# A graph network of four layers on one core: 0/1 matrices kept for a second pass, a bias added by TensorE, and 56 scatters moved from the setup into layer 0

## The chip, the cores and the metric

The kernel runs on one core of a Trainium2 chip. The core has TensorE (PE; PEld is its weight load), VectorE (DVE), ScalarE (ACT), GpSimd (POOL) and SyncE (SP). Each engine runs its own queue of instructions in order, and semaphores join the queues. SP, ACT and POOL also issue DMAs. The metric is the device time in microseconds; three runs of the kernel before took 3559.20, 3574.22 and 3567.95 us, with a median of 3567.95 us. In what follows, a time such as "at 655.5" is counted from the start of the one profiled execution.

## What is computed

A network of four graph layers works on 50000 nodes with 64 features and 25000 edges that are sorted by target. Each layer normalises x, applies a ReLU and adds its result to x:

```python
edge_index = jnp.stack([src, dst])
h = jnp.maximum(_layernorm(x, axis=-1), 0.0)
x = x + _L0_gnn_ref(h, edge_index, ...)      # relu(cat(h[src], h[dst]) @ W_msg + b_msg), mean by target, update
h = jnp.maximum(_layernorm(x, axis=-1), 0.0)
x = x + _L1_gnn_ref(h, edge_index, ...)      # normalised sum by target, then a linear layer
h = jnp.maximum(_layernorm(x, axis=-1), 0.0)
x = x + _L2_gnn_ref(h, edge_index, edge_type_8, ...)   # attention by target, then a hidden layer
h = jnp.maximum(_layernorm(x, axis=-1), 0.0)
x = x + _L3_gnn_ref(h, src, dst, edge_weight, ...)     # exp(-t L) h, a Taylor series of sparse products by source
```

Layers 0, 1 and 2 sum over the edges of a target. Layer 3 sums over the edges of a source, so the kernel also needs the edges ordered by source.

## The kernel before

All work is in `fast` (L974). Nodes are handled in NQ = 49 blocks of 1024 (8 columns of 128 nodes). Edges are held 128 to a tile, in NT = 196 tiles. The kernel is written in a tile framework: tiles come from pools, and the framework puts the instructions of every engine into an order of its own. It takes what it expects to be ready first and, of several, what stands first in the program; it also adds the semaphores. So work that stands late in the program can run early: layer 0's first normalisations run at 4 us, ahead of the setup that stands before them. A pool that is opened after another was closed gets its memory, and its tiles wait until that memory is free.

The setup goes through these stages.

- **Pass 1** (L1285 to L1294), once per edge tile: `block_hot` (L1272) compares the tile's source blocks `sblk` with a row of numbers and gives a 0/1 matrix `bh` of 128 x 392 in fp16; two smaller 0/1 matrices follow. Three matmuls add them up to counts per node and per block. `otab` then says which nodes have outgoing edges.
- **Gathers** (L1323): for each of the 196 tiles GpSimd fetches, with one indirect DMA, a flag from `otab` into column 3 of `raw`.
- **Pass 2** (L1374 to L1383): `block_hot` makes the same 0/1 matrix again, two matmuls (L1378, L1380) put the rank of every edge among those of its block into PSUM (`pz`, three buffers), and one DVE operation (L1382) picks the edge's own value into `slot`. From that comes `pf`, the place of every edge in the table `stab`, which is ordered by source.
- **Scatters** (L1402, by the helper at L1018): for each of the 196 tiles GpSimd writes 128 rows of 64 bytes of `raw` to their places `pf` in `stab`, with one indirect DMA.
- **Layer 0's tables** (`layer0_tables`, L1162), a pipeline of three stages over the 49 blocks: `norm` loads and normalises x (L1146 to L1152; ScalarE squares at L1151 and takes roots at L1139), `turn` transposes h on TensorE (L1181), copies it out of PSUM (L1183) and stores it as `h0t`; `product` multiplies by both halves of W_msg into PSUM (`pab`, four buffers, L1196). ScalarE copies one half of the result to `at` (L1197). DVE adds the message bias to the other half (L1198), and `pack` splits it into three bf16 parts (L1099 to L1102). The results go to `atab` (from SP, L1201) and `btab` (from ACT, L1202).
- **The degree work** (L1426 to L1496), mostly on DVE: edge positions `nrs`, keys, degrees of targets, checks.

Then the pools of the setup are closed. `weights` (L2035) loads and prepares the weights of the later layers, and **layer 0** (L2161 to L2229) runs as a pipeline of six stages over the 49 blocks: `fetch` gathers five tiles of `ga` from `atab` on GpSimd (four buffers) and loads `bt`, `cat`, `xt` and `keys` on SP; `hots` builds 0/1 matrices on DVE; `message`, `sums`, `update` and `project` follow. The bias of the update enters by a matmul with three rows of ones (L2005, `bias_in`).

Beside layer 0 runs a generator, `itertools.chain(weights(), load_slots())`. `Pace` (L121) takes 0.1 of a step from it after each stage of each block. `load_slots` (L1906) reads `stab` back in five loads and copies four columns; from these the later lists for layer 3 are built (`lists_pace`, from L1748 on). These lists begin at the end of layer 0. After layer 0 come layers 1, 2 and 3, and at the end GpSimd adds the last terms into `out` (L2720).

Of the kernel before, what the change touches and what calls it, by code (L numbers as in the profile page):

```python
# [23 lines left out]
F16 = mybir.dt.float16  # L24
BF16 = mybir.dt.bfloat16
I32 = mybir.dt.int32
# [43 lines left out]
W3 = ((0, 0), (0, 1), (0, 1), (0, 2), (0, 2), (1, 2), (1, 3), (1, 3), (2, 4), (2, 4), (2, 5), (3, 5), (3, 5), (3, 5))  # L70
SECOND = 3
NKEPT = 14
LEV = 1 << 16
FAR = 1 << 20
NORM = 1.0
# [898 lines left out]
def fast(ctx: ExitStack, tc: tile.TileContext, a: dict, out: bass.AP, flag: bass.AP):  # L974
# [42 lines left out]
    def scatter(tab, src, idx, last):  # L1017
        return nc.gpsimd.indirect_dma_start(  # L1018
            out=tab[:, :], out_offset=IndirectOffsetOnAxis(ap=idx, axis=0),
            in_=src, in_offset=None, bounds_check=last, oob_is_err=False)  # L1020
# [27 lines left out]
    def row_bcast(name, n=D, pool=const):  # L1048
        t = pool.tile([P, n], F32, name="b_" + name)
        src = a[name]  # L1050
        nc.scalar.dma_start(t, bass.AP(tensor=src.tensor, offset=src.offset, ap=[[0, P], [1, n]]))
        return t
# [25 lines left out]
    def along(row, n):  # L1078

        return row[:, None, :].to_broadcast([P, n, row.shape[1]])  # L1080
# [23 lines left out]
    def stacked(pool, src, n, w, name):  # L1104

        x3 = pool.tile([3 * n, 1, 3, w], F32, name=name + "_x")
        nc.vector.tensor_copy(x3[:, 0, 0, :], src)
        h = split(x3)
        which = pool.tile([3 * n, 3], F32, name=name + "_w")
        o = pool.tile([3 * n, w], F32, name=name + "_o")  # L1110
        nc.vector.memset(o, 0.0)
        for k in range(3):

            nc.vector.tensor_scalar(which[:, k:k + 1], pidx[:3 * n], float(k * n), None, op0=OP.is_ge)
            if k < 2:
                nc.vector.tensor_scalar(o[:, 0:1], pidx[:3 * n], float(k * n + n), None, op0=OP.is_lt)
                nc.vector.tensor_mul(which[:, k:k + 1], which[:, k:k + 1], o[:, 0:1])
        nc.vector.tensor_scalar(o, h[:, 0, 0, :], which[:, 0:1], None, op0=OP.mult)
        for k in (1, 2):
            nc.vector.scalar_tensor_tensor(o, h[:, 0, k, :], which[:, k:k + 1], o, op0=OP.mult, op1=OP.add)  # L1120
        b = pool.tile([3 * n, w], BF16, name=name)
        nc.vector.tensor_copy(b, o)
        return b
# [38 lines left out]
    def layer0_tables(hook):  # L1162
        with tc.tile_pool(name="pac", bufs=1) as cp, tc.tile_pool(name="pa", bufs=3) as pool, \
                tc.tile_pool(name="ppa", bufs=1, space=PSUM) as ps:
            wab = cp.tile([P, 2 * D], F32, name="wab")
            for h in range(2):
                for i in range(2):
                    nc.scalar.dma_start(wab[h * D:(h + 1) * D, i * D:(i + 1) * D],
                                        a["L0_gnn_W_msg"][i * D:(i + 1) * D, :])
            bmsg = row_bcast("L0_gnn_b_msg", pool=cp)  # L1170

            def norm(q, s):
                xt = pool.tile([P, 8, D], F32, name="xt")
                load_x(xt, q)
                s.h = pool.tile([P, 8, D], F32, name="h")
                norm_relu(pool, s.h, xt)

            def turn(q, s):
                pt = ps.tile([P, 4, P], F32, name="pt", bufs=2)
                for i in range(4):  # L1180
                    nc.tensor.transpose(pt[:, i, :], s.h[:, 2 * i:2 * i + 2, :].rearrange("p a d -> p (a d)"), ident)  # L1181
                s.tr = pool.tile([P, 4, P], F32, name="tr")
                nc.scalar.activation(s.tr, pt, AF.Copy)  # L1183
                for h in range(2):
                    nc.scalar.dma_start(
                        h0t[:, 1024 * q:1024 * q + 1024].rearrange("f (i h n) -> f h i n", i=4, h=2)[:, h],
                        s.tr[h * D:(h + 1) * D])

            def product(q, s):
                at = pool.tile([P, 8, D], F32, name="at")  # L1190
                b3 = pool.tile([P, 8, 3, D], F32, name="b3")
                for h in range(2):
                    pab = ps.tile([P, 4, 2 * D], F32, name="pab", bufs=4)
                    for i in range(4):
                        r = slice(h * D, h * D + D)
                        nc.tensor.matmul(pab[:, i, :], s.tr[r, i, :], wab[r, :], start=True, stop=True)  # L1196
                    nc.scalar.activation(at[:, h::2, :], pab[:, :, :D], AF.Copy)  # L1197
                    nc.vector.tensor_add(b3[:, h::2, 0, :], pab[:, :, D:], along(bmsg, 4))  # L1198
                bt = pool.tile([P, 8, BW], BF16, name="bt")
                pack(b3, bt.rearrange("p b (k d) -> p b k d", k=3))  # L1200
                nc.sync.dma_start(nodes(atab, q), at)  # L1201
                nc.scalar.dma_start(nodes(btab, q), bt)  # L1202

            pipeline(range(NQ), (norm, turn, product), hook)


# [9 lines left out]
    with tc.tile_pool(name="emp", bufs=1) as pool:  # L1216
        none = pool.tile([P, NQ, PW], I32, name="none")
        nc.vector.memset(none, 0)
        nc.vector.memset(none[:, :, 0:1], -1)
        for tab, n in [(stab, TL)] + [(lrow[k], c) for k, c in CAP.items() if k > 3]:  # L1220
            for t in range(0, n, NQ):
                m = min(NQ, n - t)
                nc.scalar.dma_start(tab.rearrange("(p t) f -> p t f", p=P)[:, t:t + m, :], none[:, :m, :])

    with tc.tile_pool(name="so", bufs=1) as sp, tc.tile_pool(name="sw", bufs=4) as sw:
        def load_e(name, dt, pad):
# [42 lines left out]
        nc.vector.memset(spike, 0.0)  # L1269
        nc.vector.memset(spike[:, HT2 - 1:HT2], 1.0)  # L1270

        def block_hot(t):  # L1272
            b = sw.tile([P, BK], F16, name="bh")
            nc.vector.tensor_scalar(b, it16[:, :BK], sblk[:, t:t + 1], None, op0=OP.is_equal)
            return b

# [89 lines left out]
        with tc.tile_pool(name="ps2", bufs=2, space=PSUM) as ps:  # L1366
            st = block_slots(outd, ps, "s")
            for i in range(2):
                pp = ps.tile([HT2, BK], F32, name="pp")
                if i:  # L1370
                    nc.tensor.matmul(pp, ones[:HT2, :HT2], hist[:, 0, :], start=True, stop=False)
                nc.tensor.matmul(pp, above[:HT2, :HT2], hist[:, i, :], start=(i == 0), stop=True)
                nc.vector.tensor_add(pre16[:, i, :], pp, st[:HT2, :])
            for t in range(NT):  # L1374
                h, u = divmod(t, HT2)
                b = block_hot(t)
                pz = ps.tile([P, BK], F32, name="pz", bufs=3)
                nc.tensor.matmul(pz, ident16[:HT2, u:u + 1].to_broadcast([HT2, P]), pre16[:, h, :],  # L1378
                                 start=True, stop=False)
                nc.tensor.matmul(pz, above16, b, start=False, stop=True)  # L1380
                junk = sw.tile([P, BK], F32, name="junk", bufs=2)
                nc.vector.scalar_tensor_tensor(junk, rowi[:, :BK], sblk[:, t:t + 1], pz, op0=OP.is_equal,  # L1382
                                               op1=OP.mult, accum_out=slot[:, t:t + 1])  # L1383

        nc.vector.tensor_scalar(slot, slot, 0.0, float(FAR), op0=OP.max, op1=OP.min)
        si, s1, s2 = (sp.tile([P, NT], I32, name=f"slot{i}") for i in range(3))
# [12 lines left out]
        nc.vector.scalar_tensor_tensor(s2, srct, float(N), s2, op0=OP.is_ge, op1=OP.max)  # L1399
        pf = sp.tile([P, NT], I32, name="pf")  # L1400
        nc.vector.scalar_tensor_tensor(pf, s2, float(FAR), s1, op0=OP.mult, op1=OP.add)
        for t in range(NT):  # L1402
            put = scatter(stab, raw[:, t, :], pf[:, t:t + 1], P * TL - 1)
            if t:
                tc.declare_no_dep(put.ins, group="slots", reason="rows are distinct")
            tc.add_to_no_dep_group("slots", put.ins)


        rl = sp.tile([NQ, RW, 3], I32, name="rl")
# [493 lines left out]

    cols = [lw.tile([P, BK], I32, name=f"lcol{i}")[:, :TL] for i in range(4)]

    def load_slots():  # L1906

        for t0 in range(0, TL, NQ):
            part = lw.tile([P, NQ, PW], I32, name="lpart")
            nc.sync.dma_start(part, stab.rearrange("(p t) f -> p t f", p=P)[:, t0:t0 + NQ, :])  # L1910
            yield
            for i, c in enumerate(cols):
                nc.vector.tensor_copy(c[:, t0:t0 + NQ], part[:, :, i])
        nc.vector.tensor_scalar(skey.rearrange("p (q i) -> p q i", i=5), rowi[:, :NQ, None].to_broadcast([P, NQ, 5]),
                                -1024.0, None, op0=OP.mult)
        nc.vector.tensor_add(skey, skey, cols[0])
        nc.vector.tensor_copy(swgt.bitcast(I32), cols[2])
        nc.vector.tensor_copy(sptr, cols[1])
        yield
# [241 lines left out]
    with tc.tile_pool(name="l0c", bufs=1) as cp, tc.tile_pool(name="l0", bufs=2) as pool, \  # L2161
# [61 lines left out]
            nc.scalar.dma_start(nodes(x1tab, q), s.x1)  # L2223
            nc.sync.dma_start(nodes(g1tab, q), g)

        work = Pace(itertools.chain(weights(), load_slots()), 0.1)
        next(work.work)
        lists_pace.edge = 5.0
        pipeline(range(NQ), (fetch, hots, message, sums, update, project), work, lists_pace, False)  # L2229
# [557 lines left out]
```

## Time and profile before

| what | value |
|---|---|
| median of three runs | 3567.95 us |
| the profiled execution | 3569.77 us |
| its span, first to last instruction | 3568.0 us |
| mean granted TensorE clock | 0.693 |
| DVE busy | 2620.7 us (73%) |
| PE busy | 2492.4 us (70%) |
| POOL busy | 2070.2 us (58%) |
| ACT busy | 1328.5 us (37%) |
| pass 1 | 22 to 131 us |
| pass 2 | 138 to 314 us |
| layer 0's tables | 314 to 587 us |
| degree work on DVE | 587 to 647.5 us |
| layer 0, first message matmul | 684.7 us |
| first use of the lists' columns | 1094.6 us |

Lines of the profile are read so. A row of the stretches view has the stretch and its length, then for each engine the busy time and, in brackets, the number of instructions; then the granted TensorE clock (1.00 is full), the share of the DMA engines that was busy, and GB/s. A line of the timeline has the start, the duration, the engine, the line of the program, the operation, `out<-in`, the shape and the number of merged instructions; a bracket at its end gives the idle time before it and what ended that. "q" behind an engine (SPq, ACTq) marks the engine's sequencer, which issues DMAs. In the view of a tile the three durations of a group are the least, the median and the greatest, in ns. The busy slices of the page cut the span in 40 equal parts of 89 us; a digit is the busy share in tenths.

### The profile page before, as it was taken

The numbers are of one execution on the slowest core, as the hardware profiler recorded it, in microseconds if no ns is written. First come the engines' busy times: TensorE is split into PE (matmuls) and PEld (weight loads), VectorE is DVE, ScalarE is ACT, GpSimd is POOL, SyncE is SP. The second block draws the span as 40 slices with busy tenths as digits, with TensorE's granted clock in tenths as the row PEclk, the third lists the DMA queues.
The fourth block names the chain that finished last, engine by engine and source line by source line (L and its number), as shares of the span: only waits on it lengthen the run. The fifth ranks groups of instructions, "written<-read, shape, count | busy, mean of one in ns | idle before, by whom it ended". The sixth has DMA issues, their size and how long they took to land. (4 is left out here: it accounts for less than half of the span.)

```text
span 3568.0 us, 62333 instructions
## 1 busy us (share of the span) xinstructions
PE 2492.4 (70%) x21184; PEld 1729.4 (48%) x21184; DVE 2620.7 (73%) x8434; ACT 1328.5 (37%) x2962; POOL 2070.2 (58%) x1955
## 2 busy tenths in 40 slices
PE   7898675399987673477669779889888554356620
PEld 3324565266665452355446445555554443356520
DVE  9999998699998882488677877777878576456410
ACT  0002553144442262377204326646667333333000
POOL 0377777655550477665374127665430787775786
PEclk9755555699996575688657667777779775567555
DMA  1003783487771362478654234343233646377221
GB/s 54 6 4 90 205 234 123 110 224 212 211 200 44 90 197 75 130 234 243 188 145 124 62 90 132 111 122 110 80 94 101 211 139 193 96 216 213 45 26 12
DMA packets 530638, 463.35 MB, mean 130 GB/s; under 512 B 281171, under 2 KB 387954, under 8 KB 530180
## 3 DMA queue, kind: packets, MB, share of 16 engines
q1 hardware_dynamic: 365012, 269.33, 26.5%
q10 hardware_dynamic: 93408, 139.47, 11.3%
q0 software_dynamic: 71888, 50.46, 7.6%
q8 instruction: 169, 2.77, 0.3%
q14 instruction: 161, 1.32, 0.1%
HBM read 226.23 MB, written 233.89 MB: 129 GB/s over the span
## 5 line engine op out<-in xcount | busy, mean ns | idle before, releaser
L1013 POOL DMA_INDIRECT kvg<-kvtab,nrs x245 | 260.6, 1064 | 307.6 <-DVE es L2329 184.0
L1013 POOL DMA_INDIRECT gt<-g1tab,nrs x245 | 243.6, 994 | 238.6 <-DVE lhot L1791 110.6
L1013 POOL DMA_INDIRECT y<-h3tab,sptr x245 | 276.8, 1130 | 138.9 <-issue 68.0
L1013 POOL DMA_INDIRECT ga<-atab,nrs x245 | 250.3, 1022 | 170.4 <-DVE z L2190 60.5
L1991 PEld LDWEIGHTS <-soh 128*128 128x128 bf16 x4410 | 221.7, 117 | 237.0 <-issue 221.8
L1013 POOL DMA_INDIRECT raw<-otab,nrd x196 | 193.4, 987 | 191.9 <-DVE bad L1159 132.5
L1981 PE MATMUL pa<-soh,m 128*64 128x256 bf16 (+3 forms) x1764 | 238.9, 348 | 25.2 <-DVE m L1093 11.6
L1018 POOL DMA_INDIRECT stab<-raw,pf x196 | 207.3, 1058 | 59.8 <-issue 59.8
L1013 POOL DMA_INDIRECT lgot<-nmap,ldst x183 | 190.1, 1039 | 75.3 <-issue 52.8
L1991 PE MATMUL po<-g,soh 128*128 128x64 bf16 x2205 | 123.3, 215 | 145.5 <-DVE g L1093 143.0
L1950 DVE TENSOR_SCALAR soh<-it,key 128x512 bf16<-128x512 f16 (+2 forms) x735 | 210.7, 332 | 1.8 <-PE pa L1981 1.6
L1991 PE MATMUL po<-y,soh 128*128 128x64 bf16 x2205 | 122.3, 228 | 125.9 <-DVE y L1093 65.4
L2272 PE MATMUL pp<-wkv,tr 64*128 64x256 f32 x784 | 151.2, 496 | 52.4 <-ACT tr L2001 52.1
L1013 POOL DMA_INDIRECT y<-ftab,ldst x140 | 138.9, 992 | 75.0 <-issue 45.7
L1093 DVE TENSOR_TENSOR y<-y 128x320 f32<-128x320 f32 (+1 forms) x196 | 75.6, 389 | 140.6 <-ACT y L2617 116.3
L1942 DVE TENSOR_SCALAR noh<-keys,pblk 128x256 bf16<-128x256 f16 (+1 forms) x784 | 176.0, 286 | 2.8 <-DMA keys<-ktab 2.7
L1196 PE MATMUL pab<-wab,tr 64*128 64x128 f32 x784 | 150.3, 437 | 32.5 <-ACT tr L1183 32.5
L1981 PEld LDWEIGHTS <-m 128*64 128x64 bf16 x1764 | 118.0, 119 | 97.9 <-issue 32.5
L1196 PEld LDWEIGHTS pab<-wab,tr 64*128 64x128 f32 x784 | 136.3, 324 | 51.5 <-ACT tr L1183 51.5
L2338 PE MATMUL pe<-qt,noh 128*128 128x64 bf16 x2205 | 157.7, 231 | 0.3 <-DVE noh L1942 0.2
L2720 POOL DMA_INDIRECT out<-y,lnode x85 | 132.4, 1558 | 38.3 <-issue 24.4
L2617 ACT ACTIVATE y<-y,swgt 128x64 f32<-128x64 f32 x245 | 82.2, 345 | 176.6 <-DMA y<-h3tab,sptr 161.1
(607 smaller groups left out, 7496.8 us busy)
## 6 DMA issues: line engine op xcount, KB each, us to landing
kvtab<-kv SPq DMA_DIRECT2D x49, 512.0 KB
ftab<-f ACTq DMA_DIRECT2D x98, 256.0 KB
xt<-in_x SPq DMA_DIRECT2D x96, 256.0 KB
btab<-bt ACTq DMA_DIRECT2D x49, 384.0 KB
bt<-btab SPq DMA_DIRECT2D x49, 384.0 KB
qtab<-qt ACTq DMA_DIRECT2D x49, 384.0 KB
qt<-qtab SPq DMA_DIRECT2D x49, 384.0 KB
xs<-xstab SPq DMA_DIRECT2D x70, 256.0 KB
```

Of the source, the lines that this page charges most:

```text
L1013: return nc.gpsimd.indirect_dma_start(out=dst, out_offset=None, in_=tab[:, :], in_offset=IndirectOffsetOnAxis(ap=idx, axis=0))
L1018: return nc.gpsimd.indirect_dma_start(out=tab[:, :], out_offset=IndirectOffsetOnAxis(ap=idx, axis=0), in_=src, in_offset=None, bounds_chec ...
L1093: nc.vector.tensor_sub(x3[:, :, k, :], x3[:, :, k - 1, :], h[:, :, k - 1, :])
L1196: nc.tensor.matmul(pab[:, i, :], s.tr[r, i, :], wab[r, :], start=True, stop=True)
L1942: nc.vector.tensor_scalar(s.noh[:, j, :n * P], s.keys[:, t0 * P:(t0 + n) * P], pblk[:, j:j + 1], None, op0=OP.is_equal)
L1950: nc.vector.tensor_scalar(oh[:, OHW[i]:OHW[i + 1]], it16[:, b0 * P:(b0 + n) * P], keys[:, q, i:i + 1], None, op0=OP.is_equal)
L1981: nc.tensor.matmul(o, l, r, start=(k == 0), stop=(k == len(t) - 1))
L1991: nc.tensor.matmul(po[:, j, :], oh[:, c:c + P], msg[:, i, k, :], start=(not started and i == t0 and k == 0), stop=(end and (not started or ...
L2272: nc.tensor.matmul(pp[:, i, :], s.tr[r, 2 * k + i, :], wkv[r, :], start=True, stop=True)
L2338: nc.tensor.matmul(pe[:, i, :], s.noh[:, j, c:c + P], s.qt[:, j, k, :], start=False, stop=(j == b0 + nb - 1 and k == 2))
L2617: nc.scalar.activation(y3[:, i, 0, :], s.y[:, i, :], AF.Copy, scale=swgt[:, 5 * q + i:5 * q + i + 1])
L2720: st = nc.gpsimd.indirect_dma_start(out=out[:, :], out_offset=IndirectOffsetOnAxis(ap=s.node[:, t:t + 1], axis=0), in_=sums[k][:, t, :], i ...
```

## The change

Three things are changed.

1. `block_hot` keeps its matrix in pass 1 for the first HELD = 112 tiles, in one tile `held` of 128 x 112 x 392 fp16, and pass 2 takes it from there. The memory is given back after pass 2, before layer 0's tables are opened.
2. In the tables the message bias is put into PSUM by one matmul per half block: three rows of ones times three bf16 rows of the bias, with zeros in the half that gets none. The four products of the half block are added to it, and ScalarE copies the result to `b3` in place of DVE's addition. The bias rows are prepared by `stacked` (L1104), a memset and a copy.
3. Of the 196 scatters into `stab`, the setup issues 140. The rows and places of the last LATER = 56 tiles are stored to DRAM by two DMAs on ACT's queue. `load_slots` loads them again on SP, at the start, into layer 0's memory, issues the 56 scatters one for each step, and only then reads `stab`. The pace goes from 0.1 to 0.34 of a step.

```diff
+HELD = 112
+LATER = 56
...
-            bmsg = row_bcast("L0_gnn_b_msg", pool=cp)
+            b1 = stacked(cp, row_bcast("L0_gnn_b_msg", pool=cp)[:3, :], 1, D, "bmsg")
+            bmsg = cp.tile([3, 4, 2, D], BF16, name="bmsg4")
+            nc.vector.memset(bmsg, 0.0)
+            nc.vector.tensor_copy(bmsg[:, :, 1, :], b1[:, None, :].to_broadcast([3, 4, D]))
+            bmsg = bmsg.rearrange("p b k d -> p (b k d)")
...
                     pab = ps.tile([P, 4, 2 * D], F32, name="pab", bufs=4)
+                    nc.tensor.matmul(pab.rearrange("p b d -> p (b d)"), ones3, bmsg, start=True, stop=False)
                     for i in range(4):
                         r = slice(h * D, h * D + D)
-                        nc.tensor.matmul(pab[:, i, :], s.tr[r, i, :], wab[r, :], start=True, stop=True)
+                        nc.tensor.matmul(pab[:, i, :], s.tr[r, i, :], wab[r, :], start=False, stop=(i == 3))
                     nc.scalar.activation(at[:, h::2, :], pab[:, :, :D], AF.Copy)
-                    nc.vector.tensor_add(b3[:, h::2, 0, :], pab[:, :, D:], along(bmsg, 4))
+                    nc.scalar.activation(b3[:, h::2, 0, :], pab[:, :, D:], AF.Copy)
...
+    def to_slots_by_source(t, rows, places):
+        put = scatter(stab, rows, places, P * TL - 1)
+        if t:
+            tc.declare_no_dep(put.ins, group="slots", reason="rows are distinct")
+        tc.add_to_no_dep_group("slots", put.ins)
+
+    later = [dram.tile([P, LATER * n], I32, name=nm) for nm, n in (("lraw", PW), ("lpf", 1))]
...
-        def block_hot(t):
-            b = sw.tile([P, BK], F16, name="bh")
+        held_pool = ExitStack()
+        held = held_pool.enter_context(tc.tile_pool(name="held", bufs=1)).tile([P, HELD, BK], F16, name="held")
+
+        def block_hot(t, again=False):
+            if t < HELD:
+                b = held[:, t, :]
+                if again:
+                    return b
+            else:
+                b = sw.tile([P, BK], F16, name="bh")
             nc.vector.tensor_scalar(b, it16[:, :BK], sblk[:, t:t + 1], None, op0=OP.is_equal)
             return b
...
-                b = block_hot(t)
+                b = block_hot(t, True)
...
+        held_pool.close()
...
-        for t in range(NT):
-            put = scatter(stab, raw[:, t, :], pf[:, t:t + 1], P * TL - 1)
-            if t:
-                tc.declare_no_dep(put.ins, group="slots", reason="rows are distinct")
-            tc.add_to_no_dep_group("slots", put.ins)
+        for t in range(NT - LATER):
+            to_slots_by_source(t, raw[:, t, :], pf[:, t:t + 1])
+        nc.scalar.dma_start(later[0], raw[:, NT - LATER:, :].rearrange("p t f -> p (t f)"))
+        nc.scalar.dma_start(later[1], pf[:, NT - LATER:])
...
-    def load_slots():
+    def load_slots(pool):
 
+        rows, places = pool.tile([P, LATER, PW], I32, name="rows"), pool.tile([P, LATER], I32, name="places")
+        nc.sync.dma_start(rows.rearrange("p t f -> p (t f)"), later[0])
+        nc.sync.dma_start(places, later[1])
+        yield
+        for t in range(LATER):
+            to_slots_by_source(NT - LATER + t, rows[:, t, :], places[:, t:t + 1])
+            yield
...
-        work = Pace(itertools.chain(weights(), load_slots()), 0.1)
+        work = Pace(itertools.chain(weights(), load_slots(cp)), 0.34)
```

## The prediction, made before the changed kernel was run

> **What bounds the kernel now.** I read the busy slices of the page first, then the busy time of chosen stretches, then the timeline and the list of waits inside those that the change touches. The chain that ended last reaches back only to the additions into `out` (L2720) and the stage before them; the change touches nothing there. What it can move is the start of layer 0, and all later stages hang on that through x.
>
> ```profile
> DVE  9999998699998882488677877777878576456410
> POOL 0377777655550477665374127665430787775786
> PEclk9755555699996575688657667777779775567555
> ```
>
> ```profile
> core 0: us, PE busy (x) PEld busy (x) DVE busy (x) ACT busy (x) POOL busy (x), PEclk, DMA share, GB/s
> 22.00:131.00 109.00, 108.11 (x588) 47.73 (x588) 109.00 (x599) 1.24 (x3) 0.00 (x0) 1.00 0.02 5
> 152.00:314.00 162.00, 149.39 (x367) 45.24 (x365) 154.34 (x557) 1.28 (x1) 122.67 (x130) 0.50 0.03 4
> 340.00:590.00 250.00, 188.01 (x916) 159.20 (x916) 223.76 (x457) 141.48 (x313) 192.67 (x189) 0.50 0.73 215
> 590.00:655.50 65.50, 15.19 (x247) 14.61 (x247) 54.09 (x158) 1.43 (x3) 51.53 (x43) 0.50 0.03 6
> 690.00:1090.00 400.00, 366.69 (x4212) 275.07 (x4210) 381.12 (x1154) 180.87 (x455) 229.41 (x224) 0.97 0.74 208
> ```
>
> The rows are pass 1, pass 2, layer 0's tables, the degree work, layer 0. DVE paces the first two; the tables have no full engine. Layer 0 starts when two chains are done: DVE's (its last setup work at 647.5) and GpSimd's (196 gathers from 134.4 to 387.6, then 196 scatters to 654.3). The later ends the setup's memory, and all queues restart together:
>
> ```profile
> 653.35 0.97 POOL L1018 DMA_INDIRECT stab<-raw,pf  x1 [0.30 <-issue]
> 655.61 0.11 DVE L1111 MEMSET bupd_o<- 3x64 f32 x1 [8.11 <-DMA stab<-raw,pf]
> 655.59 0.57 SPq L2053 DMA_DIRECT2D wkv<-in_L_gnn_Wk  x1
> 677.05 0.36 SPq L2175 DMA_DIRECT2D bt<-btab  x1
> ```
>
> So GpSimd is the bound by only 8 us over DVE. From 655.5 to the first message matmul at 684.7 SP issues the weight loads and then layer 0's first loads; that stretch stays.
>
> **Pass 2 (saves).**
>
> ```profile
> 300.62 0.62 DVE L1382 SCALAR_TENSOR_TENSOR junk<-rowi,f_sblk,pz 128x392 f32<-128x392 f32 x1
> 301.17 0.86 DVE L1274 TENSOR_SCALAR bh<-it,f_sblk 128x392 f16<-128x392 f16 x3
> 302.15 0.62 DVE L1382 SCALAR_TENSOR_TENSOR junk<-rowi,f_sblk,pz 128x392 f32<-128x392 f32 x1
> ```
>
> Durations overlap, so I count from start to start: 0.55 us from one L1382 to the next (300.62 to 301.17), 0.98 for three 0/1 matrices, 0.327 each, 0.873 a tile. For 112 tiles L1274 goes: 112 x 0.327 = **-36.6**. Late next is TensorE, whose matmuls here (L1380) start 0.33 apart at clock 0.50, 0.66 a tile; at that the saving is 112 x (0.873-0.66) = -23.9. In pass 1 a gapless stream got clock 1.00 and 0.17 a matmul, so I take -36.6.
>
> **What the kept matrices push away.** `held` is 112 x 784 B = 88 KB a partition. I expect the table stage's tiles to get that memory only after its last read. Before, DVE did six reductions, six scalings and three subtractions for the first blocks while it waited at the start:
>
> ```profile
> 3.99 0.69 DVE L1146 TENSOR_REDUCE ln_s<-xt 128x8 f32<-128x512 f32 x1 [1.22 <-DMA xt<-in_x]
> ```
>
> At 0.60, 0.10 and 0.60 apart that is **+6** on DVE's path (0 if the memory does not collide). The bias rows need some 18 small DVE operations; like those of `bupd` (0.05 to 0.1 apart) **+2**.
>
> **Tables (unclear sign).** DVE loses 98 additions L1198, 0.375 apart: 37 us. ScalarE gains 98 copies of 0.38: 141 of 250 busy becomes 178, hidden while PSUM copies do not stand ahead of the turn copy L1183; if they do, 0.38 a block, 19 us. TensorE gains 98 matmuls. Its steady rhythm:
>
> ```profile
> 539.93 3.09 PE L1196 MATMUL pab<-wab,tr 64*128 64x128 f32 x16 [0.69 <-ACT tr L1183]
> 542.96 1.11 PE L1181 MATMUL pt<-ident,h 128*128 128x128 f32 x4
> 544.76 3.10 PE L1196 MATMUL pab<-wab,tr 64*128 64x128 f32 x16 [0.69 <-ACT tr L1183]
> ```
>
> 4.82 us a block, 49 x 4.82 = 236 of the stage's 273; in the rest TensorE waited for DVE's h (33 us by the waits). A bias matmul has this shape in layer 0:
>
> ```profile
> L2005 PE MATMUL po<-bupd,ones x49: 371/385/601, 664.2 to 1151.2; 3*128 3x512 bf16 x49
> ```
>
> A block's two cost from 0 (in the 0.69 gap) to 1.20 (the cold maximum). I take 0.385 each, half hidden: 49 x 0.385 = +19. DVE's lost work gives back some of TensorE's 33 us; I take 15, since DVE's long reciprocals and scans still stand in its queue. Net **+4**.
>
> At clock 0.50 these matmuls are dear. The Trainium skill, "TensorE: Matmul & The Clock Gate", Part 1, says the clock rises to full after about 3.4 us of sustained work; our row has 0.50 at 75% busy. With the rule the second rival below would become the forecast, 3508 in place of 3538.
>
> **GpSimd and queues.** Setup keeps 140 scatters at (654.3-387.6)/196 = 1.361: 387.6 + 190.5 = 578, no longer last. DVE's chain ends at 647.5-36.6+6+2+4 = 622.9, so the release moves from 655.5 to 622.9: **-32.6**. ScalarE's queue gets two stores of the last 56 tiles, which wait for the last gather (387.6) and hold the table work behind them; 0 if they are queued about when the gathers end.
>
> **Layer 0.** 56 scatters come into GpSimd's queue among 245 gathers, about two a block after the rows are loaded:
>
> ```profile
> 809.50 0.94 POOL L1013 DMA_INDIRECT ga<-atab,nrs  x1 [0.30 <-issue]
> 812.88 1.42 POOL L1013 DMA_INDIRECT ga<-atab,nrs  x1 [2.44 <-DVE noh L1942]
> ```
>
> It waits 2.0 to 2.4 us a block for a free buffer, 100 us between 700 and 1100, and the scatters need 56 x 1.361 = 76. The gathers are up to four blocks ahead. I take **+3**; if the scatters do not fall into the waits, a block takes 5 x 1.31 + 2.07 x 1.361 = 9.4 instead of 8.6, 27 blocks, +21. DVE, 95% busy there, gets nothing. SP gets two loads; the five loads of the slot table now wait on SP for the last scatter, with layer 0's loads behind them, covered by four buffers. Before they were issued by 962, and the lists begin at 1094.6: room.
>
> Sum: -32.6 + 3 = -29.6. The profiled execution took 3569.8 (span 3568.0 and 1.8 around it): 3540. The median of the runs is 1.8 lower, so **3538**.
>
> **Rivals.**
> - *TensorE becomes the tables' bound at half clock.* For: 188 of 250 busy at 0.50, a rhythm with 0.69 spare. With both matmuls added, 4.82+0.77 = 5.59, x 49 = 274, and 15 us of waits: 289, +16; at 0.60 each, 6.02, 295 and 10: +32. Total 3558 to 3574. Against: DVE's 37 us.
> - *TensorE fills up and gets the full clock.* Pass 1 shows the state, 690 to 1090 too. Then transfers bound the tables: a block moves 1.18 MB (x in, h0t, atab, btab; 256, 256, 256 and 384 KB in the list of DMA issues), at the 245 GB/s seen from 400 to 440 that is 4.8 us, 236 in all, -37 instead of +4: 3497. With three quarters of that I price it at 3508. GpSimd's 578 is the floor, 3495. Against: 0.50 for 250 us on end.
> - *The stores block ScalarE* (slower). Place: its queue, before the tables. If they stand ahead of the first table work, that begins at 390 and not at 285: 390+277+60 = 727, +72 on the release, 3643. It is slower than before once ScalarE idles over 30 us. Against: DVE's free 2.6 us at 631.6 was not filled by the L1111 and L2166 memsets that wait for the scatters, so the planned order does not count on GpSimd much earlier than it is. The Trainium skill, "DMA: Bandwidth & Descriptors", on the anatomy of one DMA, says that a transfer's semaphore wait is held by the issuing sequencer, which speaks for this rival; here ACT's loads L2012 stood until 655.62.
> - *GpSimd bounds layer 0*: 3538+18 = 3556.
>
> **Chances.** Forecast 0.40 (3524 to 3554); full clock 0.24; TensorE bound 0.20; blocked ScalarE 0.07; GpSimd 0.09. The range 3500 to 3582 leaves out the slower cases (0.10) and the fast end of the full clock (some 0.06). Half a per cent, about what a measurement can tell from no change, is 18 us. Faster: 0.37 + 0.24 + 0.02 = 0.63. Slower: 0.06 of the block and 0.04 of a TensorE bound with further stalls = 0.10. Same: 0.27.
>
> **What would show it.** L1382 0.55 apart for 112 tiles and the tables starting near 285; a table rhythm near 5.0 us (over 5.6 or under 4.7 is a rival); the last setup scatter near 578; all queues restarting near 623 on DVE and not on GpSimd; layer 0 at 8.6 us a block. It is wrong if ScalarE stands before 390, or if the lists wait for the slot table.

## The result and the profile after

The changed kernel is **slower**: 3732.9 us (median of 4 runs, 3718.4 to 3733.6) against 3568.7 of the kernel before, ratio 1.045 [1.043, 1.047]. The forecast was 3538, range 3500 to 3582. The profiled execution took 3718.4 us, 148.6 more than that of before; it is the fastest of the four, the others took 3732 to 3734 us. On some chips the kernel before itself took 4680 to 4749 us; every ratio below is with runs of the kernel before on the same chip.

Most of pass 2's gain is there. The busy slices (DVE, POOL, PEclk) and the same stretches as before: pass 1, pass 2, a new one, the tables.

```profile
DVE  9990577776799878248867787787878667556410
POOL 0477770057665146766547313757531378766786
PEclk9955555578899757668855766777778775567555
```

```profile
core 0: us, PE busy (x) PEld busy (x) DVE busy (x) ACT busy (x) POOL busy (x), PEclk, DMA share, GB/s
22.00:131.00 109.00, 106.54 (x580) 46.89 (x579) 109.00 (x601) 1.88 (x4) 1.15 (x1) 1.00 0.01 3
152.00:272.00 120.00, 108.56 (x337) 36.67 (x335) 116.50 (x425) 0.00 (x0) 90.74 (x97) 0.71 0.07 10
279.00:392.00 113.00, 1.86 (x4) 0.41 (x4) 0.69 (x3) 0.00 (x0) 85.40 (x91) 0.50 0.03 6
395.00:690.00 295.00, 252.63 (x1065) 179.39 (x1067) 213.88 (x407) 176.66 (x434) 135.94 (x125) 0.50 0.69 194
```

The fourth slice of DVE is 0: from 279 to 392 us DVE and TensorE work 0.69 and 1.86 us, ScalarE nothing. Only GpSimd goes on, with its gathers and the first scatters. ScalarE's timeline says why ("q" marks its DMA issues):

```profile
197.80 2.50 ACTq L1170 DMA_DIRECT2D wab<-in_L_gnn_W_msg  x4
200.34 0.59 ACTq L1053 DMA_DIRECT2D b_L_gnn_b_msg<-in_L_gnn_b_msg  x1
376.67 0.33 ACTq L1429 DMA_DIRECT2D lraw<-raw  x1
392.13 0.33 ACTq L1430 DMA_DIRECT2D lpf<-pf  x1
392.50 0.63 ACT L1153 ACTIVATE ln_sq<-ln_xc 128x512 f32<-128x512 f32 x1 [264.65 <-DMA rl<-fields]
```

The two stores stand ahead of the tables' first square. The first goes at 376.7, after the last gather (issued at 374.0); the second 15.5 us later, which the profile puts down to SP's `rl` loads. SP's queue was held too: 58 of its 98 `rl` loads were out by 225, then it stood 153.3 us, put down to the first store, and went on at 379.2. Before, these loads ran from 133.6 to 253.7 without such a stop. Why loads on SP wait for that store is not shown. DVE waits behind ScalarE:

```profile
393.16 0.69 DVE L1140 TENSOR_REDUCE ln_v<-ln_sq 128x8 f32<-128x512 f32 x1 [113.47 <-ACT ln_sq L1153]
```

A second hole is in layer 0. SP issues nothing for 64 us, while `keys`, `xt` and `bt` of the next blocks stand behind the first load of the slot table (SP's timeline):

```profile
878.80 0.39 SPq L2206 DMA_DIRECT2D bt<-btab  x1
879.52 1.10 SPq L2060 DMA_DIRECT2D cat<-h0t  x2
944.32 0.33 SPq L1941 DMA_DIRECT2D lpart<-stab  x1
944.74 0.39 SPq L1966 DMA_DIRECT2D keys<-ktab  x1
945.21 0.38 SPq L1070 DMA_DIRECT2D xt<-in_x  x1
```

The last scatter was issued at 942.2. In the order of GpSimd's queue the 56 late scatters do not stand two a block, but 2, 10, 12, 12, 12 and 8 between the gathers of one block and the next, so that the gathers of five blocks lie 18, 23, 22, 22 and 17 us apart.

The ledger, in us of the profiled executions. The restart is the first weight load on SP, the rest is all that comes after layer 0's last message matmul:

| | before | after | difference |
|---|---|---|---|
| pass 2, first to last pick of a slot | 138.1 to 313.3 | 133.3 to 271.5 | 175.2 to 138.2: -37.0 |
| tables, first to last product | 318.6 to 583.9 | 397.6 to 691.4 | 265.3 to 293.8: +28.5 |
| last scatter of the setup | 653.4 | 567.7 | |
| restart | 655.6 | 754.6 | +99.0 |
| first message matmul | 684.7 | 784.9 | **+100.2** |
| layer 0, first to last message matmul | 439.0 | 494.1 | **+55.1** |
| rest of the span | 2444.3 | 2437.6 | -6.7 |

The last row is not read as an effect: in the profiles of the eight kernels that ran on chips of this kind it lies between 2427 and 2455 us.

### The profile page after: what moved, and what is told of

The parts are those of the page before. It is cut to its first block, busy times and chain, and to the rows that moved or that the text cites. A ratio compares the mean times of both kernels' runs of the same rounds, so it can differ in the third digit from the quotient of the medians.

```text
span 3716.6 us, 62517 instructions
## 1 busy us (share of the span) xinstructions
PE 2516.1 (68%) x21282; PEld 1737.3 (47%) x21282; DVE 2561.4 (69%) x8241; ACT 1350.2 (36%) x3060; POOL 2047.0 (55%) x1955
## 5 line engine op out<-in xcount | busy, mean ns | idle before, releaser
L1015 POOL DMA_INDIRECT raw<-otab,nrd x196 | 185.7, 947 | 187.3 <-DVE st_s L1370 127.9
L1140 DVE TENSOR_REDUCE ln_v<-ln_sq 128x8 f32<-128x512 f32 x147 | 99.9, 681 | 201.1 <-ACT ln_sq L1153 200.7
L1153 ACT ACTIVATE ln_sq<-ln_xc 128x512 f32<-128x512 f32 x147 | 92.0, 626 | 341.3 <-DMA rl<-fields 264.7
L1020 POOL DMA_INDIRECT stab<-raw,pf x140 | 151.1, 1079 | 42.6 <-issue 42.6
```

The costliest lines, as they stand in the source:

```text
L1015: return nc.gpsimd.indirect_dma_start(out=dst, out_offset=None, in_=tab[:, :], in_offset=IndirectOffsetOnAxis(ap=idx, axis=0))
L1020: return nc.gpsimd.indirect_dma_start(out=tab[:, :], out_offset=IndirectOffsetOnAxis(ap=idx, axis=0), in_=src, in_offset=None, bounds_chec ...
L1140: nc.vector.tensor_reduce(v, sq, AX.X, OP.add)
L1153: nc.scalar.activation(sq, xc, AF.Square)
```

## The experiments

**Theory.** ScalarE's queue (113 us of idling), SP's wait with GpSimd's bunched scatters (55), and the bias in the tables (22 to 28, put down to TensorE's matmuls) lost far more than pass 2 gained. The rivals are stated with each run.

### Stores off ScalarE's queue

```diff
-        nc.scalar.dma_start(later[0], raw[:, NT - LATER:, :].rearrange("p t f -> p (t f)"))
-        nc.scalar.dma_start(later[1], pf[:, NT - LATER:])
+        nc.gpsimd.dma_start(later[0], raw[:, NT - LATER:, :].rearrange("p t f -> p (t f)"))
+        nc.gpsimd.dma_start(later[1], pf[:, NT - LATER:])
```

> The kernel with the two stores on GpSimd's queue and the late scatters as the changed kernel has them, where the kernel before takes about 3575 us. The tied kernel took 3562. If the bunched scatters and SP's wait behind them make the stall of layer 0, this one has it again: 35 to 45 us more, 3597 to 3607 us. Rival (the stall of the changed kernel came from something that the late tables brought): no stall, within 8 us of 3562.

Measured: 3604.8 us (two runs, 3597.2 and 3612.4), ratio 1.0096 [1.0059, 1.0132] to a kernel before of 3567.2. ScalarE's timeline:

```profile
200.14 0.59 ACTq L1053 DMA_DIRECT2D b_L_gnn_b_msg<-in_L_gnn_b_msg  x1
278.55 0.63 ACT L1153 ACTIVATE ln_sq<-ln_xc 128x512 f32<-128x512 f32 x1 [150.70 <-DVE ln_xc L1151]
```

The first square comes at 278.6 and no longer at 392.5, and waits for DVE, which comes from pass 2. The restart comes at 633.7: the stores' place alone cost 754.6 - 633.7 = **121 us**. Memory did not hold the tables until 392: SP issued the first `xt` loads at 197.6, once the last kept matrix had been read. SP's `rl` loads have no stop here. Layer 0 still takes 492.3 us, so its stall is independent of the late tables.

### Slot-table loads off SP's queue as well

```diff
-            nc.sync.dma_start(part, stab.rearrange("(p t) f -> p t f", p=P)[:, t0:t0 + NQ, :])
+            nc.gpsimd.dma_start(part, stab.rearrange("(p t) f -> p t f", p=P)[:, t0:t0 + NQ, :])
```

> The same with the five loads of the slot table on GpSimd's queue, so that the wait for the last scatter no longer stands on SP ahead of layer 0's loads; the scatters stay bunched. If SP's wait alone makes the stall: near the tied kernel, 3560 to 3567 us. If the bunched scatters starve layer 0 through GpSimd's queue: 25 to 45 us above it, 3587 to 3607 us.

Measured: 3586.2 us, ratio 1.0043 [1.0027, 1.0058], on the chip of the run before. Layer 0 takes 478.0 us: 14 of the 53 are SP's wait, 39 stay. They are four blocks of 13.5, 20.8, 22.5 and 17.1 us by their stores of `g1tab`, against 8.6 otherwise: 73.9 - 34.4 = 39.5. There GpSimd is the bound; its own waits between 740 and 840 are the 0.3 us before each DMA (the three largest groups):

```profile
POOL stab L1020 <- issue: 13.4, 44, 0.3
POOL ga L1015 <- issue: 8.8, 29, 0.3
POOL ga L1015 <- DMA ga<-atab,nrs: 0.6, 2, 0.3
```

SP's wait alone did not make the stall; the bunched scatters are the larger part.

### Scatters tied to the gathers

The stores on GpSimd's queue, the slot-table loads on SP again, and each late scatter placed behind the gathers that precede it in the program:

```diff
+            with tc.issue_after(fetched[-1].ins):
+                to_slots_by_source(NT - LATER + t, rows[:, t, :], places[:, t:t + 1])
...
-                gather(s.ga[:, i, :], atab, nrs[:, q, i:i + 1])
+                fetched.append(gather(s.ga[:, i, :], atab, nrs[:, q, i:i + 1]))
```

> The kernel with the two stores on GpSimd's queue, and the late scatters tied: each may not stand in GpSimd's order ahead of the gathers of layer 0 that precede it in the program, so that two stand between the gathers of two blocks and not ten to twelve. Where the kernel before takes 3568 us: if the bunching starves layer 0, its stall goes from 50 us to under 15 and the time is 3560 to 3565 us, 35 to 40 below the kernel with the bunched scatters; rival (the wait on SP for the last scatter alone): the wait moves to the place of the last scatter and stays, within 10 us of that kernel's 3600. Where the kernel before takes over 4700 us, the same differences against 4745.

Measured: 3562.3 us, ratio 0.9964 [0.9936, 0.9992] to a kernel before of 3577.8. Layer 0 takes 459.8 us. I first took the 21 us over 439 for GpSimd's two scatters a block, since that is the price of the prediction's worse case. SP's timeline shows another place:

```profile
931.93 0.32 SPq L2258 DMA_DIRECT2D g1tab<-g  x1
...
941.09 0.32 SPq L2258 DMA_DIRECT2D g1tab<-g  x1
...
945.68 0.33 SPq L1969 DMA_DIRECT2D keys<-ktab  x1
973.12 0.33 SPq L1944 DMA_DIRECT2D lpart<-stab  x1
973.54 0.38 SPq L2209 DMA_DIRECT2D bt<-btab  x1
974.02 0.82 SPq L2258 DMA_DIRECT2D g1tab<-g  x1
```

Up to 941 the blocks take 9.0 to 9.2 and 8.2 us in turn, 8.65 on average, almost as before (8.6): two scatters a block fit. Then SP stands 27 us before the first load of the slot table. The blocks after it are 32.9, 6.1 and 6.6 us apart, 45.6 for three and not 25.8: +19.8, nearly the whole loss.

### The kept matrices alone

Bias on DVE, all 196 scatters in the setup, the old pace.

```diff
-LATER = 56
+LATER = 0
...
```

> Only the kept matrices, all 196 scatters in the setup, bias on DVE, the old pace; the kernel before at about 3577. If GpSimd's chain of gathers and scatters is the bound, which pass 2 does not shorten: the last scatter near 650, restart 5 to 10 us earlier, 3567 to 3573 us. Rival (the chain moves with pass 2, since the places come 40 us earlier): 3537 us.

Measured: 3563.3 us, ratio 0.9991 [0.9974, 1.0008]. The timeline at the restart:

```profile
650.00 0.97 POOL L1020 DMA_INDIRECT stab<-raw,pf  x1 [0.30 <-issue]
652.23 0.56 SPq L2069 DMA_DIRECT2D wkv<-in_L_gnn_Wk  x1
652.24 0.11 DVE L1113 MEMSET bupd_o<- 3x64 f32 x1 [42.56 <-DMA stab<-raw,pf]
```

DVE has been idle for 42.6 us when GpSimd's last scatter ends, 34.5 more than before the change (8.1): nearly all that pass 2 gains turns into a wait for GpSimd. The scatters must leave the setup for pass 2 to count.

### Kept in SBUF, tied, bias on DVE

The last 24 tiles are gathered into a tile that outlives the setup, so there is neither a store nor a load; the places are copied by one DVE operation.

```diff
+LATER = 24
...
+            gather(raw[:, t, 3:4] if k < 0 else rows[:, k, 3:4], otab, nrd[:, t:t + 1])
...
+        nc.vector.tensor_copy(places, pf[:, NT - LATER:])
...
```

> A kernel made from the findings: matrices kept for 112 tiles, bias on DVE, 24 tiles scattered late from a tile that is kept in SBUF (no stores and no loads), tied to the gathers of layer 0, two a block. If the bias matmuls make the tables 297 us long, they take 276 here, DVE is done near 617 and the last of 172 scatters ends near 624: the restart comes near 625 and the time is 25 to 33 us below the kernel before, 3544 to 3552 where that takes 3577. Rival (the tables are as long without the bias matmuls, since something else bounds them): restart near 638, 3558 to 3566 us.

Measured: 3546.4 us, ratio 0.9932 [0.9905, 0.9959], below the kernel before (3567.2 here). Tables 280.1 to 545.2 = 265.1 us, as long as before the change; restart at 619.4. With the bias on TensorE they took 286.8 (stores on GpSimd's queue). The stretch from 400 to 540 us, first with the bias on TensorE, then without:

```profile
400.00:540.00 140.00, 130.60 (x549) 91.95 (x547) 102.40 (x196) 89.77 (x222) 109.23 (x102) 0.50 0.77 213
```

```profile
400.00:540.00 140.00, 107.59 (x520) 90.78 (x520) 124.31 (x255) 80.71 (x181) 107.71 (x107) 0.50 0.76 217
```

With the bias on TensorE that engine is 93% busy and without it 77%, at a clock of 0.50 in both. It looks like the bound; its timeline with the bias (stores on GpSimd's queue) is close to gapless:

```profile
500.84 3.09 PE L1203 MATMUL pab<-wab,tr 64*128 64x128 f32 x16 [0.15 <-ACT tr L1189]
503.86 0.60 PE L1200 MATMUL pab<-bmsg,ones 3*128 3x512 bf16 x1
504.58 1.12 PE L1187 MATMUL pt<-ident,h 128*128 128x128 f32 x4
505.63 0.60 PE L1200 MATMUL pab<-bmsg,ones 3*128 3x512 bf16 x1
506.38 3.09 PE L1203 MATMUL pab<-wab,tr 64*128 64x128 f32 x16 [0.15 <-ACT tr L1189]
```

506.38 - 500.84 = 5.54 us a block, where it was 4.82: two bias matmuls of 0.60, of which one fits into the gap where TensorE waits for the turn copy (0.69 before, 0.15 left). But ScalarE's queue is as full. Its three stores a block are issued there, and the next root comes only when they are out:

```profile
506.36 0.58 ACTq L1191 DMA_DIRECT2D h0t<-tr  x1
507.12 0.47 ACTq L1209 DMA_DIRECT2D btab<-bt  x1
507.64 0.60 ACTq L1191 DMA_DIRECT2D h0t<-tr  x1
508.29 0.30 ACT L1141 ACTIVATE ln_v<-ln_v,epsc 128x8 f32<-128x8 f32 x1 [1.44 <-issue]
```

Of the 140 us ScalarE is busy for 89.8, stands 31.3 in this way and waits 18 for other engines; with the bias on DVE it waits 57. This run takes the matmuls and the copies away together, so it cannot say which of the two made the tables longer. Copies without matmuls follow further down.

### The wait on SP taken away

The kernel just shown, with the five loads of the slot table six blocks later in SP's order.

```diff
+        for _ in range(12):
+            yield
...
+            with tc.issue_after(loaded[-1].ins):
+                nc.sync.dma_start(part, stab.rearrange("(p t) f -> p t f", p=P)[:, t0:t0 + NQ, :])
...
+            loaded.append(nc.sync.dma_start(s.bt, nodes(btab, q)))
```

> The kernel with 24 late scatters at two a block, and the five loads of the slot table six blocks later in SP's order (tied to a block's own load on SP), so that the last scatter is long done when SP comes to the first of them. Seen so far in that kernel, where the kernel before takes 3567 us: the blocks with two scatters run at 8.6 us as without, and the one loss of layer 0 is 7 to 10 us where SP stands 13 us at the first load. If SP's wait is all that the late scatters cost, layer 0 goes from 449 to 439 to 441 us and the time from 3546 to 3536 to 3539, 28 to 31 below the kernel before. Rival (the scatters themselves cost 0.4 us each, the loss only comes out later): layer 0 stays near 449, 3544 to 3550 us.

Measured: **3536.9 us**, ratio 0.9895 [0.9872, 0.9917] to a kernel before of 3570.4: the best of all. SP's timeline has no hole at the first load, and the blocks around it stay 8.2 and 9.0 apart:

```profile
843.17 0.32 SPq L2254 DMA_DIRECT2D g1tab<-g  x1
845.40 0.54 SPq L1940 DMA_DIRECT2D lpart<-stab  x1
...
851.36 0.32 SPq L2254 DMA_DIRECT2D g1tab<-g  x1
...
860.34 0.32 SPq L2254 DMA_DIRECT2D g1tab<-g  x1
```

Layer 0 takes 444.0 us, against 448.7 with the wait. Of the 8 to 10 expected 5 came back. The time fell within what was expected, but its interval and that of the kernel with the wait overlap a little, so the pair is told apart by the timeline rather than by the times. The two profiled executions even stand the other way round (3534.3 with the wait, 3543.0 without): a restart 3 us later and a rest of the span of 2444.2 against 2434.0 hide the 5.

### Runs on chips with a slower setup

Twelve runs fell on chips where the kernel before takes 4680 to 4749 us. There the setup is another one. DVE's timeline of pass 2 with the stores on GpSimd's queue:

```profile
303.32 0.62 DVE L1406 SCALAR_TENSOR_TENSOR junk<-rowi,f_sblk,pz 128x392 f32<-128x392 f32 x1 [4.96 <-remote]
308.92 0.62 DVE L1406 SCALAR_TENSOR_TENSOR junk<-rowi,f_sblk,pz 128x392 f32<-128x392 f32 x1 [4.97 <-remote]
```

A tile takes 5.6 us while GpSimd gathers (until 378 us), and pass 2 ends at 505; the gathers are then long done, so that a store that waits for them holds nobody. What is tested of the stores and of layer 0 is hidden, and all ratios lie between 0.995 and 1.004. The first four, on one chip:

> The changed kernel with one edit: the two stores of the last 56 tiles are issued from GpSimd's queue, where they stand behind the gathers anyway, and no longer from ScalarE's. Queue theory (ScalarE stood before the tables because the store of raw waits for the last gather): the tables begin near 281 us in place of 395 and, at their 295 us, end near 576; with the 61 us from there to the restart of all queues, that comes near 637; the stall of layer 0 around 880 to 944 stays at about 50 us; 3600 us. Rival (the tables began late because their tiles wait for memory, that of the kept matrices, or for SP's loads): they still begin near 395, 3715 to 3735 us.

> The kernel with the two stores on GpSimd's queue, and the message bias added by DVE again as before the change. Theory (the two bias matmuls of a block make TensorE the bound of the tables at half clock): the tables take 276 us as before and not 295, so 19 us less than the kernel with the stores on GpSimd's queue, near 3581 us. Rival (the longer tables come from elsewhere, DVE's additions cost as much as TensorE's matmuls): within 5 us of that kernel, near 3600.

> The kernel with the two stores on GpSimd's queue, and the five loads of the slot table issued from GpSimd's queue too, so that the wait for the last scatter no longer stands on SP ahead of layer 0's loads. Theory (SP's wait alone makes the stall of layer 0): the stall of 50 us shrinks to 5, near 3555 us. Rival (the planned order puts 10 to 12 scatters between the gathers of two blocks, so GpSimd needs 22 us a block for five blocks and layer 0 starves on the gathers): 25 to 45 us of the stall stay, 3577 to 3597 us.

> Only the first part of the change: the 112 kept matrices, all 196 scatters in the setup, bias on DVE, the old pace. Theory (pass 2 gives its 42 us on DVE's chain, and GpSimd's 196 gathers and scatters are the bound): DVE done near 608, the last scatter near 645, the restart 8 to 12 us earlier than before, 3557 to 3560 us. Rival (GpSimd's chain moves with DVE's, since pf comes 42 us earlier and scatters begin earlier): 3526 us.

Measured 1.0025 [1.0005, 1.0045], 0.9988 [0.9967, 1.0009], 1.0029 [1.0013, 1.0044] and 0.9953 [0.9933, 0.9973]. The second does tell something: it took 4719.2 us and the first 4741.9, 22.7 less where 19 were expected, and its tables take 428.5 us from first to last product, not 453.1. So the bias costs as much here as elsewhere. Why the kept matrices alone gain 0.5% here is open. The first again, on another chip: 1.0037 [1.0010, 1.0065].

> The kernel with the two stores on GpSimd's queue a second time, because the first time the kernel before itself took 4726 us on that chip, with waits of 5 us between engines all through pass 2, where it takes 3568 elsewhere. Where the kernel before takes about 3568: queue theory: tables from 281 to 576, restart near 637, the stall of layer 0 stays at 50, 3600 us. Rival (tiles wait for memory or for SP's loads): 3715 to 3735 us.

Two more questions met only such chips. One scatter a block in place of two:

```diff
-        work = Pace(itertools.chain(weights(), load_slots(cp)), 0.34)
+        work = Pace(itertools.chain(weights(), load_slots(cp)), 0.17)
```

> The kernel with 24 late scatters from the kept tile, at half the pace (0.17 of a step), so that one scatter stands between the gathers of two blocks and not two. GpSimd waits 2.0 to 2.4 us a block in layer 0, which has room for one scatter of 1.3 us and not for two. If that wait decides what a late scatter costs, layer 0 (first to last message matmul) goes from 449 us back to the 439 to 441 of the kernel before, and the time from 3546 to about 3537 us, with the kernel before at 3567. Rival (a late scatter costs its 0.4 us of layer 0 wherever it stands, or the later slot table holds up the lists): 3544 to 3556 us.

> The kernel with 24 late scatters at one a block once more, since the first time the kernel before took 4731 us on that chip, where pass 2 waits 5 us a tile and the setup hides all that is tested here. Where it takes about 3567: if GpSimd's wait of 2.0 to 2.4 us a block has room for one scatter and not for two, layer 0 goes from 449 us to 439 to 441, and the time is about 3537 us. Rival (a late scatter costs its 0.4 us wherever it stands, or the later slot table holds up the lists): 3544 to 3556 us.

> The kernel with 24 late scatters at one a block, a third time, for a chip where the kernel before takes about 3570 us. There: if GpSimd's wait of 2.0 to 2.4 us a block has room for one scatter and not for two, layer 0 goes from 449 us to 439 to 441, and the time is about 3537 us. Rival (a late scatter costs its 0.4 us wherever it stands, or the later slot table holds up the lists): 3544 to 3556 us.

> The kernel with 24 late scatters at one a block, for a chip where the kernel before takes about 3570 us. There: if GpSimd's wait of 2.0 to 2.4 us a block has room for one scatter and not for two, layer 0 goes from 449 us to 439 to 441, and the time is about 3537 us, 30 below the kernel before. Rival (a late scatter costs its 0.4 us wherever it stands, or the later slot table holds up the lists): no more than 20 below it.

Measured 1.0014 [0.9989, 1.0038], 1.0003 [0.9988, 1.0017], 1.0007 [0.9992, 1.0022] and 0.9991 [0.9974, 1.0008]. The reason given there, that GpSimd's wait has no room for two scatters, had fallen by then to the pace of 8.6 us with two. And copies without matmuls (the message bias left out):

```diff
-                    nc.tensor.matmul(pab.rearrange("p b d -> p (b d)"), ones3, bmsg, start=True, stop=False)
```

> The tied kernel without the 98 bias matmuls, but with ScalarE's copies in place of DVE's additions: the message bias is left out of the computation. It tells TensorE's matmuls from ScalarE's copies, since both came with the change. If the matmuls lengthen the tables (5.55 us a block with them against 4.82 before): the tables take 265 us and not 287, the restart comes near 613, 3540 us where the tied kernel took 3562. If ScalarE's copies stand ahead of the copy of the turned block and hold TensorE: the tables stay above 280 us, 3556 to 3565 us.

> The tied kernel without the bias matmuls but with ScalarE's copies, again, for a chip where the kernel before takes about 3570 us; the message bias is left out of the computation. If TensorE's matmuls lengthen the tables: 265 us of tables and not 287, 3540 us where the tied kernel took 3562. If ScalarE's copies do it by standing ahead of the copy of the turned block: tables above 280 us, 3556 to 3565 us.

> The tied kernel without the bias matmuls but with ScalarE's copies, for a chip where the kernel before takes about 3570 us; the message bias is left out of the computation. If TensorE's matmuls lengthen the tables: 265 us of tables and not 287, restart near 613, 3540 us where the tied kernel took 3562. If ScalarE's copies do it by standing ahead of the copy of the turned block: tables above 280 us, 3556 to 3565 us.

Measured 0.9999 [0.9971, 1.0027], 0.9972 [0.9947, 0.9997] and 0.9973 [0.9934, 1.0012]. There is no tied kernel on such a chip to set these times against, but the traces answer the question. From 700 us on GpSimd is idle there, and the tables run as on the other chips. The median from one block's first product to the next, in us:

| the message bias | other chips | these chips, from 700 us on |
|---|---|---|
| added by DVE | 4.82 to 4.83 | 4.83 |
| matmuls on TensorE, copies on ScalarE | 5.56 | 5.49 to 5.54 |
| copies on ScalarE, no matmuls | not run | 5.43 to 5.52 |

TensorE's timeline with the copies alone (the second of the three):

```profile
804.01 3.09 PE L1202 MATMUL pab<-wab,tr 64*128 64x128 f32 x16 [0.69 <-ACT tr L1189]
807.73 1.09 PE L1187 MATMUL pt<-ident,h 128*128 128x128 f32 x4 [0.63 <-DVE h L1154]
809.50 3.09 PE L1202 MATMUL pab<-wab,tr 64*128 64x128 f32 x16 [0.69 <-ACT tr L1189]
813.25 1.08 PE L1187 MATMUL pt<-ident,h 128*128 128x128 f32 x4 [0.66 <-DVE h L1154]
815.03 3.09 PE L1202 MATMUL pab<-wab,tr 64*128 64x128 f32 x16 [0.69 <-ACT tr L1189]
```

TensorE is 73% busy and waits twice a block, and the block still takes 5.5 us. From first to last product the tables take 449.2, 445.9 and 447.0 us without the matmuls, 451.2 to 453.1 with them and 428.5 with DVE's additions. So most of what the bias costs comes with ScalarE's copies in place of DVE's additions; on top of them the matmuls add 2 to 7 of some 24 us. What the matmuls would cost without the copies is not shown. The likely reason is ScalarE's full queue: of 100 us (800 to 900, the first of the three) it is busy for 63.0, stands 26.7 while its stores are issued and waits 10.5 for other engines, where with DVE's additions it waits 42. DVE in turn waits 25.7 for x, whose load stands on SP behind the store of `at`, and that waits for the copies; so the order on SP may have its part. No run takes these two apart.

## Why the prediction was wrong

- **Pass 2**: right. -36.6 predicted, -37.0 measured (0.54 us from pick to pick). TensorE's clock rose from 0.50 to 0.71 there, so the lesser -23.9 at 0.50 did not come.
- **The kept matrices' memory**: right in kind. The early work moved behind pass 2; pass 1 and 2 came 4.8 us earlier for it, and the first table product came 12.4 us after pass 2 (283.7 - 271.3, stores on GpSimd's queue) and not 5.3. Net +2 where +6 was taken.
- **The two stores on ScalarE's queue, "0 if they are queued about when the gathers end"**: this is the step that failed. They were queued right after the loads of `wab` and the bias, ahead of all table work, and cost 121 us. The rival that ends slower named place and mechanism, at a chance of 0.07. The evidence against it was DVE's unfilled 2.6 us at 631.6, which is about scatters in the setup's last microseconds and says nothing on where two stores land in ScalarE's order. It also put the release at 727 (390 + 277 + 60); it came at 754.6: ScalarE was free at 392.5, the last product came 299 us later and the restart 63 after that.
- **The tables, net +4**: +21.5 (286.8 against 265.3, stores on GpSimd's queue). The term that failed is ScalarE's copies, put at 0 as "hidden" and at 19 us otherwise. With the copies and no bias matmuls a block still takes 5.43 to 5.52 us and not 4.83, so they were not hidden. The matmuls were mis-sized too: 0.60 us each and not 0.385, which is a time from layer 0 at a clock of 0.97, where the tables have 0.50; yet they add only 2 to 7 us. The rival of a TensorE bound at half clock, +16 to +32 and 5.59 a block, met the size by luck: the pace stays when its matmuls are gone. The rival of a full clock fell: 0.50 at 93% busy.
- **GpSimd no longer last**: right with the stores moved (last setup scatter 580, predicted 578). The restart at 633.7 missed 622.9 by 11: the tables were 17.5 longer than taken, the rest 6.7 shorter.
- **Layer 0, +3**: wrong by 52. "About two a block" was not what the queue got; bunched, the scatters cost 39 us. "Covered by four buffers" was wrong for the slot-table loads: SP stood 64 us and four buffers last some 34; that added 14. At two a block the scatters themselves cost nothing in the blocks' pace.
- The parts together: 121 - 22 (the restart without the stores' wait, 633.7 against 655.6) + 55 - 7 = 147 of the 148.6 between the profiled executions.

## What to carry to other kernels

A DMA that waits holds everything that is queued behind it on the engine that issues it (here ScalarE for 113 us, SP for 64): price each added DMA by the time until its last input lands, minus the time at which it stands in its queue, and put it on the queue that does the waited-for work anyway. Look at each queue's order, not at the program's: an instruction issued "one per step" may be bunched or pulled ahead. An engine's busy share leaves out the time in which it issues DMAs: ScalarE was 64% busy in the tables with the copies, and its queue 87% taken. A gain on one chain counts only to the next chain's end; here kept matrices alone gave nothing that could be measured (0.9991) until the other chain was cut as well.

## What was not expected of the hardware

- TensorE's granted clock stayed at 0.50 through 140 us at 93% busy in the tables; in pass 1 it had 1.00 at 98%. The Trainium skill, "TensorE: Matmul & The Clock Gate", Part 1, has the full clock come after about 3.4 us of sustained work. The tables' rows do not agree: 0.50 throughout, with no idle of TensorE over 0.15 us in the 5.5 us of its timeline shown.
- On some chips engines that hand work to each other take 5.6 us a tile (0.54 elsewhere) while GpSimd issues indirect DMAs, which themselves keep their 1.25 us. What "remote" waits for there is open.
